# The last twelve batches of an adapter kernel, written as one list

## Chip, core and metric

The kernel runs on one core of a Trainium2 chip. The metric is the device time of one execution in microseconds (us). Five engines work beside each other, each through its own instructions in order: TensorE (PE; its weight loads are listed as PEld), VectorE (DVE), ScalarE (ACT), GpSimd (POOL), and SyncE (SP), which here issues DMA transfers. SBUF and PSUM are the core's memories: matrix products land in PSUM, GpSimd works on SBUF.

## What is computed

x has 128 batches of 128 rows and 512 columns, float32. Each batch has an id from 0 to 9 that picks its weights:

```python
h = relu(x[b] @ W1[id] + b1[id])          # 512 -> 128
y = x[b] + h @ W2[id] + b2[id]            # 128 -> 512, and the residual
n = (y - mean(y)) * rsqrt(var(y) + 1e-5)  # by row, over 512 columns
out[b] = x[b] + n * gamma[id] + beta[id]
```

## The kernel before

One batch is one tile of 128 x 512. The tables (W1, W2, and beta, gamma, b2 spread over 128 partitions as `beta_b`, `gamma_b`, `b2_b`) stay in SBUF. A batch goes through these steps; the names are those of the helpers and lines in the profile:

- TensorE transposes x in four pieces into PSUM (`transpose_x`, L271); ScalarE copies the result to SBUF (`copy_xT`, L275).
- ScalarE copies the batch's W1 out of the table into a tile (`stage_w1`, L262). Only the first 17 batches load theirs from memory by id instead (`load_first`, L161).
- TensorE makes h (`down`, L294), ScalarE adds b1 and clamps (`relu`, L302), TensorE makes h @ W2 into one of five PSUM tiles `py` (`up`, L311).
- GpSimd adds x and b2 ahead of time (`add_b2`, L281, tile `r`) and x and beta into the output tile `o` (`add_beta`, L288). For a few batches b2 comes in another way: by VectorE (L321), or by a matmul of a selecting row with the table's parts in front of the up (`b2_by_matmul`, L310: 0, 1, 126, 127).
- VectorE adds `r` or x to `py` and sums the rows (`residual`, L328). ScalarE turns the sum into a negative mean (L342) and makes the sum of squares (`square`, L351), then a first reciprocal root (`root`, L361). VectorE improves it by a Newton step in three small operations (`rstd` 1 to 3: L365, L367, L370).
- VectorE subtracts the mean and multiplies by gamma in place (`scale`, L394), and multiplies by the reciprocal root and adds `o` (`finish`, L403). SP stores two batches at once (`store`, L407).

The small steps are done for a pair of batches at a time. The tile of the root of a pair lies in PSUM, and so do those of the last four batches, which have their own (`of_one`).

Every instruction goes through `keep`, which ties it to the one issued before on its engine, so the order of the calls is the order on each engine. The loop over `i` writes that order: iteration `i` transposes batch i, makes the down of i - 1 and the up of i - 2, and does the row statistics of b = i - 3, the scaling of the pair before, and the end of the one before that. E is 123. From b = E on `tail` writes the order by hand: batches 123, 124 and 125 end by ScalarE and GpSimd instead of VectorE (`by_pool`: ScalarE scales into a tile `n`, L450; GpSimd multiplies by gamma, L452, where VectorE has not, and adds `o`, L454), and 126 and 127 end on VectorE (L461), the last in two halves. The stores of 124 and 125 are issued in halves by ScalarE, the others by SP (L457). The kernel's last instructions are at L675.

Of the kernel before, what the change touches and what calls it, by code (L numbers as in the profile page):

```python
# [22 lines left out]
U = 2  # L23
# [3 lines left out]
def cond_resid_kernel(ctx: ExitStack, tc: tile.TileContext, x, itok, W1, b1, W2, b2, gamma, beta, out):  # L27
# [286 lines left out]
    def col(tiles, b):  # L314

        return tiles[b // 2][:, b % 2 : b % 2 + 1]
# [46 lines left out]
    def newton(n, ssq, t, u):  # L363
        if n == 1:
            keep(nc.vector.scalar_tensor_tensor(u, ssq, EPS * H3, t, ALU.add, ALU.mult))  # L365
        else:
            keep(nc.vector.scalar_tensor_tensor(u, u, 1.0 / H3, t, ALU.mult, ALU.mult))  # L367

    def newton_3(rstd, t, u):
        keep(nc.vector.scalar_tensor_tensor(rstd, u, -3.0, t, ALU.add, ALU.mult))  # L370
# [28 lines left out]
    def finish(b):  # L399
        g, j = divmod(b, 2)  # L400
        o = os[g][:, j, :]
        keep(
            nc.vector.scalar_tensor_tensor(o, ys.pop(b), rstds[g][:, j : j + 1], o, ALU.mult, ALU.add)  # L403
        )

    def store(g):
        keep(nc.sync.dma_start(out=out[2 * g : 2 * g + 2].rearrange("b s h -> s b h"), in_=os.pop(g)))  # L407
        del rstds[g]

    def on(b):  # L410
        return 0 <= b < B
# [3 lines left out]
    shifts = {}  # L415
    halves = slice(0, H // 2), slice(H // 2, H)

    def of_one(b):
        if -b not in parts_of:
            pool, tag = {E + 3: (p_h, "h"), E + 4: (p_x, "xT")}.get(b, (p_s, "s"))  # L420
            parts_of[-b] = pool.tile([P, 1], FP, tag=tag, name=f"root_of_{b}"), st.tile([P, 1], FP, tag="part", name=f"part_of_{b}")
        return parts_of[-b]

    def rstd_of(b, n):

        t, u = of_one(b)
        if n < 3:
            newton(n, ssqs[b], t, u)
        else:
            rstds[b] = st.tile([P, 1], FP, tag="rstd", name=f"rstd_{b}")  # L430
            newton_3(rstds[b], t, u)

    def deviation_of(b):
        ssqs[b] = st.tile([P, 1], FP, tag="ssq", name=f"ssq_{b}")
        sq = tp.tile([P, H], FP, tag="sq", name=f"sq_{b}")
        keep(nc.scalar.activation(sq, ys[b], AF.Square, bias=col(sums, b), scale=-float(H), accum_out=ssqs[b]))  # L436
        root(ssqs[b], of_one(b)[0])

    def rstd_col(b):
        return rstds[b] if b > E else rstds[b // 2][:, b % 2 : b % 2 + 1]  # L440

    def shift(b):
        shifts[b] = st.tile([P, 1], FP, tag="shift", name=f"shift_{b}")
        keep(nc.vector.tensor_scalar(shifts[b], col(nmeans, b), rstd_col(b), None, ALU.mult))

    def by_pool(b, scaled, cols=slice(0, H)):

        n = rp.tile([P, H], FP, tag="r", name=f"n_{b}")[:, cols]
        bias = 0.0 if scaled else shifts[b]
        keep(nc.scalar.activation(n, ys[b][:, cols], AF.Identity, bias=bias, scale=rstd_col(b)))  # L450
        if not scaled:
            keep(nc.gpsimd.tensor_tensor(n, n, gamma_b[:, bass.ds(lid(b, ET.Pool) * H, H)], ALU.mult))  # L452
        for part in halves if b > E else (cols,):
            keep(nc.gpsimd.tensor_tensor(os[b // 2][:, b % 2, part], n[:, part], os[b // 2][:, b % 2, part], ALU.add))  # L454

    def store_last(b, engine=nc.sync, cols=slice(0, H)):
        keep(engine.dma_start(out=out[b][:, cols], in_=os[b // 2][:, b % 2, cols]))  # L457

    def finish_cols(b, cols=slice(0, H)):
        o = os[b // 2][:, b % 2, cols]  # L460
        keep(nc.vector.scalar_tensor_tensor(o, ys[b][:, cols], rstd_col(b), o, ALU.mult, ALU.add))  # L461

    def tail(b):
        p = E // 2
        residual(b)
        if b == E + 1:
            rstd(p, 1)
            scale(E - 1)
            rstd(p, 2)
            finish(E - 2)  # L470
            store(p - 1)
            rstd(p, 3)
            deviation_of(b)
            shift(E)
            by_pool(E, False)
        elif b == E + 2:
            rstd_of(b - 1, 1)
            negative_means(b // 2)
            rstd_of(b - 1, 2)
            finish_cols(E - 1)  # L480
            store_last(E - 1)
            rstd_of(b - 1, 3)
            store_last(E)
            deviation_of(b)
        elif b == E + 3:
            left, right = slice(0, H // 2), slice(H // 2, H)
            few, most = slice(0, H // 4), slice(H // 4, H)
            shift(b - 2)
            by_pool(b - 2, False)
            residual(b + 1)  # L490
            rstd_of(b - 1, 1)
            scale(b - 1)
            rstd_of(b - 1, 2)
            deviation_of(b)
            negative_means(b // 2)
            scale(b)
            rstd_of(b - 1, 3)
            rstd_of(b, 1)
            deviation_of(b + 1)
            rstd_of(b, 2)  # L500
            by_pool(b - 1, True)
            for part in halves:
                store_last(b - 2, nc.scalar, part)
            for part in halves:
                store_last(b - 1, nc.scalar, part)
            rstd_of(b, 3)
            rstd_of(b + 1, 1)
            finish_cols(b)
            store_last(b)
            rstd_of(b + 1, 2)  # L510
            scale(b + 1)
            rstd_of(b + 1, 3)
            for cols in (left, right):
                finish_cols(b + 1, cols)
                store_last(b + 1, nc.sync, cols)


    def spin(n, width):
        idle = p_s.tile([P, H], FP, tag="s", name="idle")
# [54 lines left out]
    up(1)  # L574

    turned = 5
    for i in range(3, B + U):
        b = i - U - 1
        if b > G and b % G == 2 and b // G + 3 < NG and b // G + 3 >= 5:
            load_x(b // G + 3)  # L580
# [20 lines left out]
        g, half = divmod(b, 2)  # L601
        p = g - 1
        mine, old = 0 <= p < B // 2, 0 <= p - 1 < B // 2
        if b == E:
            add_b2(b + 3)
            add_beta(b + 1)
            add_b2(b + 4)
            for n in range(b + 2, B):
                add_beta(n)
        if b > E:  # L610
            tail(b)
        elif half == 0:
            if on(b):
                vector_b2(b)
                residual(b)
                square(b)
            if mine:
                scale(2 * p)
                rstd(p, 1)
            if old:  # L620
                finish(2 * p - 1)
                store(p - 1)
        else:
            if on(b):
                vector_b2(b)
            if mine:
                rstd(p, 2)
            if on(b):
                residual(b)
                square(b)  # L630
            if mine:
                rstd(p, 3)
                scale(2 * p + 1)
            if mine:
                finish(2 * p)
# [44 lines left out]
```

## Time and profile before

| | |
|---|---|
| median of 3 runs | 304.56 us (304.44 to 304.68) |
| the profiled execution | 304.08 us |
| its span, first to last instruction | 302.3 us |
| busy share of PE, DVE, ACT, POOL | 96%, 97%, 92%, 94% |
| mean granted clock of TensorE | 0.993 |

The profile has one execution. Its span is what the instructions cover; 1.8 us of the time lie around it. Rows of the timeline give start, duration, engine, line, operation, out<-in and count; rows of the groups give count, busy time, mean duration in ns and the engine's idle time just before; rows of the chain of waits give start, duration and what the end was waiting for at that moment; rows of the windows give for each engine the busy time and number of instructions in a stretch. Starts of consecutive instructions of one engine can lie closer than their durations, because they overlap.

### The profile page before, as it was taken

Reading aid. Unit: us, or ns where it says so; the run is one execution under the profiler, and the core shown is the slowest. Engines: PE = TensorE matmul, PEld = TensorE weight load, DVE = VectorE, ACT = ScalarE, POOL = GpSimd, SP = SyncE. Lnnn points to the kernel's source line nnn. Section 1 sums busy time; section 2 is a strip of 40 time slices with the busy share of each in tenths; the row PEclk is TensorE's granted clock in tenths of the full one; section 3 lists DMA queues with packets and bytes.
Section 4 is the critical chain, followed back from the end, with each engine's and each line's share of the span. In section 5 each row is a group of like instructions: output and inputs, shape, how many; then the busy total and the mean of one; then the engine's idle time right before and its main releaser. Section 6 shows DMA issues by size and latency. Waiting matters only on the chain.

```text
span 302.3 us, 7001 instructions
## 1 busy us (share of the span) xinstructions
PE 290.6 (96%) x1820; PEld 218.0 (72%) x1821; DVE 294.2 (97%) x784; ACT 279.6 (92%) x771; POOL 284.9 (94%) x240
## 2 busy tenths in 40 slices
PE   7899999999999999999999999999999999999980
PEld 3758787777777777777777777777777777777740
DVE  6989999999999999999999999999999999999995
ACT  5878789999999999999999999999999999999982
POOL 1299998999999999999999999999999999999995
PEclk9999999999999999999999999999999999999997
DMA  6999999986667876766678667767866666882244
GB/s 235 385 389 364 346 339 402 404 307 206 233 234 243 279 255 205 244 209 261 222 280 270 212 204 240 263 226 261 279 211 221 218 253 217 271 283 113 108 166 173
DMA packets 43929, 77.33 MB, mean 256 GB/s; under 512 B 2121, under 2 KB 8020, under 8 KB 43890
## 3 DMA queue, kind: packets, MB, share of 16 engines
q1 hardware_dynamic: 43254, 76.31, 73.5%
q10 hardware_dynamic: 636, 0.57, 0.6%
q8 instruction: 15, 0.25, 0.3%
q14 instruction: 24, 0.20, 0.2%
HBM read 43.32 MB, written 33.55 MB: 254 GB/s over the span
## 4 chain that ended last, share of the span: by engine, by line
PE 89%; DVE 5%; DMA 2%; issue 1%; ACT 1%; SPq 0%; POOL 0%; DVEq 0%; ACTq 0%; POOLq 0%
PE ph L294 36%; PE py L311 35%; PE pxT L271 18%; DMA x<-in_x_dram 2%; DVE py L394 2%; DVE py L328 1%; DVE o L403 1%; PE row L229 1%; SPq L161 0%; ACT n L450 0%; ACT sq L351 0%; ACT sq L436 0%; DVE o L461 0%; ACT w1s L262 0%; DVE rstd L370 0%
## 5 line engine op out<-in xcount | busy, mean ns | idle before, releaser
L288 POOL TENSOR_TENSOR o<-x,beta_b 128x512 f32<-128x512 f32 x128 | 170.1, 1359 | 12.7 <-DVE beta_b L247 11.6
L294 PE MATMUL ph<-xT,w1s 128*128 128x128 f32 x1024 | 135.3, 275 | 0.2 <-DMA w1s<-in_L_cond_W_dram 0.2
L281 POOL TENSOR_TENSOR r<-x,b_b 128x512 f32<-128x512 f32 x97 | 131.7, 1360 | 0.0
L311 PE MATMUL py<-w,hT 128*128 x256 | 131.3, 595 | 0.0
L294 PEld LDWEIGHTS ph<-xT,w1s 128*128 128x128 f32 x1024 | 124.8, 192 | 1.3 <-issue 0.6
L271 PEld LDWEIGHTS pxT<-ident,x 128*128 128x128 f32 x512 | 66.0, 149 | 66.8 <-issue 49.9
L394 DVE SCALAR_TENSOR_TENSOR py<-py,nmean,gamma_b 128x512 f32<-128x512 f32 x126 | 94.8, 753 | 0.0
L403 DVE SCALAR_TENSOR_TENSOR o<-py,rstd,o 128x512 f32<-128x512 f32 x122 | 91.1, 747 | 0.0
L351 ACT ACTIVATE sq<-py,sum 128x512 f32<-128x512 f32 x124 | 85.8, 692 | 0.6 <-DVE py L328 0.6
L275 ACT COPY xT<-pxT 128x512 f32<-128x512 f32 x128 | 74.7, 583 | 4.3 <-PE pxT L271 4.1
L271 PE MATMUL pxT<-ident,x 128*128 128x128 f32 x512 | 77.6, 274 | 0.8 <-DMA x<-in_x_dram 0.6
L262 ACT COPY w1s<-w 128x512 f32 x111 | 68.0, 613 | 0.0
L328 DVE SCALAR_TENSOR_TENSOR py<-py,r 128x512 f32<-128x512 f32 x97 | 66.9, 690 | 0.2
L302 ACT ACTIVATE hT<-ph,b1T 128x128 f32<-128x128 f32 x128 | 46.9, 367 | 8.8 <-PE ph L294 4.2
L311 PEld LDWEIGHTS py<-w,hT 128*128 128x128 f32 x256 | 39.1, 192 | 1.4 <-issue 0.7
L351 ACT ACTIVATION_READ_ACCUMULATOR sq<-py,sum 128x1 f32 x124 | 25.1, 202 | 0.0
L328 DVE SCALAR_TENSOR_TENSOR py<-py,x 128x512 f32<-128x512 f32 x31 | 21.7, 699 | 1.4 <-PE py L311 1.1
L321 DVE TENSOR_TENSOR py<-py,b_b 128x512 f32<-128x512 f32 x27 | 18.6, 689 | 0.1
L361 ACT ACTIVATE root<-ssq,eps 128x2 f32<-128x2 f32 x62 | 16.5, 265 | 0.0
L328 DVE DVE_READ_ACCUMULATOR py<-py,r 128x1 f32 x97 | 13.6, 140 | 0.0
L342 ACT ACTIVATE nmean<-sum 128x2 f32<-128x2 f32 x62 | 12.3, 198 | 0.0
L365 DVE SCALAR_TENSOR_TENSOR part<-ssq,root 128x2 f32<-128x2 f32 x62 | 9.3, 149 | 0.2 <-ACT root L361 0.2
(57 smaller groups left out, 81.2 us busy)
## 6 DMA issues: line engine op xcount, KB each, us to landing
out_dram<-o SPq DMA_DIRECT2D x61, 512.0 KB, 3.3
x<-in_x_dram SPq DMA_DIRECT2D x27, 1024.0 KB, 6.7
x<-in_x_dram SPq DMA_DIRECT2D x10, 512.0 KB, 7.2
w1s<-in_L_cond_W_dram SPq DMA_DIRECT2D x17, 256.0 KB, 8.7
w<-in_L_cond_W_dram SPq DMA_DIRECT2D x4, 640.0 KB, 8.2
w<-in_L_cond_W_dram SPq DMA_DIRECT2D x1, 1792.0 KB, 9.8
w<-in_L_cond_W_dram SPq DMA_DIRECT2D x1, 768.0 KB, 5.3
out_dram<-o SPq DMA_DIRECT2D x3, 256.0 KB, 2.0
```

Source lines behind the costliest of these rows:

```text
L262: keep(nc.scalar.copy(w1s[b].rearrange("p k a -> p (k a)"), src))
L271: keep(nc.tensor.transpose(pxs[b][:, k, :], cols, ident))
L275: keep(nc.scalar.copy(xT[b], pxs.pop(b)))
L281: keep(nc.gpsimd.tensor_tensor(rs[b], xb(b), b2_b[:, bass.ds(v * H, H)], ALU.add))
L288: keep(nc.gpsimd.tensor_tensor(os[g][:, j, :], xb(b), beta_b[:, bass.ds(v * H, H)], ALU.add))
L294: nc.tensor.matmul(phs[b], lhsT=w1s[b][:, k, :], rhs=xT[b][:, k, :], start=(k == 0), stop=(k == KC - 1))
L302: keep(nc.scalar.activation(hT[b], phs.pop(b), AF.Relu, bias=b1T[:, bass.ds(lid(b, ET.Activation), 1)]))
L311: keep(nc.tensor.matmul(ys[b], lhsT=hT[b], rhs=w2[:, bass.ds(v * H, H)], start=not m, stop=True))
L328: nc.vector.scalar_tensor_tensor(ys[b], ys[b], 1.0, r, ALU.mult, ALU.add, accum_out=col(sums, b))
L351: nc.scalar.activation(sq, ys[b], AF.Square, bias=col(sums, b), scale=-float(H), accum_out=col(ssqs, b))
L394: nc.vector.scalar_tensor_tensor(ys[b], ys[b], col(nmeans, b), gamma_b[:, bass.ds(v * H, H)], ALU.add, ALU.mult)
L403: nc.vector.scalar_tensor_tensor(o, ys.pop(b), rstds[g][:, j : j + 1], o, ALU.mult, ALU.add)
```

## The change

The loop stops after b = 118, and everything from the transposition of 122 on is one list of calls, 152 lines long. In it:

- b2 of 122 comes by the matmul in front of its up, not by GpSimd.
- x + beta of 126 is made by TensorE in PSUM (`base_of`: a matmul that picks beta, and one of the identity with x), not by GpSimd; batch 126 is scaled into a tile `n` in SBUF, and its end adds the PSUM tile.
- W1 of 125, 126 and 127 is loaded from memory by id (`load_late`), not copied by ScalarE.
- 118, 123, 124 and 125 are scaled by VectorE and end by ScalarE and GpSimd (`n_of`, `add_of`); 121 is not scaled by VectorE, GpSimd multiplies by gamma (`gamma_of`). Before, 118 and 121 ended on VectorE, and 123 and 124 had gamma from GpSimd.
- The root and the three Newton operations of 124 to 127 are for one batch each, as before; the root's tile lies in SBUF (`root_of`, tag "one").
- The means of 124 and 125 are made by ScalarE, those of 126 and 127 by one small VectorE operation each.
- All stores go through SP; 122 and 123 are stored as a pair, 124, 125 and 127 in halves.
- The register loads of the ids for the last two groups stand at the head of the list.

The core of the diff, with `tail` and the functions it alone used taken out, and the list whole:

```diff
-        return b in (0, 1) or b >= B - 2
+        return b in (0, 1) or b - E in (-1, 3, 4)
...
-    def of_one(b):
...
-    def by_pool(b, scaled, cols=slice(0, H)):
...
-    def tail(b):
...
+    def beta_of(b):
+        keep(nc.gpsimd.tensor_tensor(out_of(b), xb(b), beta_b[:, bass.ds(lid(b, ET.Pool) * H, H)], ALU.add))
+    def b2_of(b):
+        rs[b] = rp.tile([P, H], FP, tag="r", name=f"r_{b}")
+        keep(nc.gpsimd.tensor_tensor(rs[b], xb(b), b2_b[:, bass.ds(lid(b, ET.Pool) * H, H)], ALU.add))
     def rstd_col(b):
+        return rstds[-b] if -b in rstds else rstds[b // 2][:, b % 2 : b % 2 + 1]
     def shift(b):
         shifts[b] = st.tile([P, 1], FP, tag="shift", name=f"shift_{b}")
         keep(nc.vector.tensor_scalar(shifts[b], col(nmeans, b), rstd_col(b), None, ALU.mult))
+    def n_of(b, scaled, cols=slice(0, H)):
+        rs[b] = rp.tile([P, H], FP, tag="r", name=f"n_{b}")
         bias = 0.0 if scaled else shifts[b]
+        keep(nc.scalar.activation(rs[b][:, cols], ys[b][:, cols], AF.Identity, bias=bias, scale=rstd_col(b)))
+    def mean_of(b, engine):
+        if b // 2 not in nmeans:
+            nmeans[b // 2] = st.tile([P, 2], FP, tag="nmean", name=f"nmean_{b // 2}")
+        if engine is nc.scalar:
+            keep(nc.scalar.activation(col(nmeans, b), col(sums, b), AF.Copy, scale=-1.0 / H))
+        else:
+            keep(nc.vector.tensor_scalar(col(nmeans, b), col(sums, b), -1.0 / H, None, ALU.mult))
+    def gamma_of(b):
+        keep(nc.gpsimd.tensor_tensor(rs[b], rs[b], gamma_b[:, bass.ds(lid(b, ET.Pool) * H, H)], ALU.mult))
+    def add_of(b, cols=slice(0, H)):
+        o = out_of(b)[:, cols]
+        keep(nc.gpsimd.tensor_tensor(o, rs[b][:, cols], o, ALU.add))
+    def square_of(b):
+        ssqs[-b] = st.tile([P, 1], FP, tag="ssq", name=f"ssq_of_{b}")
+        sq = tp.tile([P, H], FP, tag="sq", name=f"sq_{b}")
+        keep(nc.scalar.activation(sq, ys[b], AF.Square, bias=col(sums, b), scale=-float(H), accum_out=ssqs[-b]))
+    def root_of(b):
+        parts_of[-b] = st.tile([P, 1], FP, tag="one", name=f"root_of_{b}"), st.tile([P, 1], FP, tag="part", name=f"part_of_{b}")
+        root(ssqs[-b], parts_of[-b][0])
+    def rstd_of(b, n):
+        t, u = parts_of[-b]
+        if n < 3:
+            newton(n, ssqs[-b], t, u)
+        else:
+            rstds[-b] = st.tile([P, 1], FP, tag="rstd", name=f"rstd_of_{b}")
+            newton_3(rstds[-b], t, u)
+    base = {}
+    def base_of(b, pool, tag):
+        base[b] = pool.tile([P, H], FP, tag=tag, name=f"base_{b}")
+        pick_b = pick[:, bass.ds(lid(b, ET.PE), 1)].to_broadcast([96, P])
+        keep(nc.tensor.matmul(base[b], lhsT=pick_b, rhs=parts[:96, :], start=True, stop=False))
+        keep(nc.tensor.matmul(base[b], lhsT=ident, rhs=xb(b), start=False, stop=True))
+    def end_of(b, cols=slice(0, H)):
+        o = out_of(b)[:, cols]
+        keep(nc.vector.scalar_tensor_tensor(o, (rs if b in base else ys)[b][:, cols], rstd_col(b), base[b][:, cols] if b in base else o, ALU.mult, ALU.add))
+    def scale_out(b):
+        v = lid(b, ET.DVE)
+        rs[b] = rp.tile([P, H], FP, tag="r", name=f"n_{b}")
+        keep(
+            nc.vector.scalar_tensor_tensor(
+                rs[b], ys[b], col(nmeans, b), gamma_b[:, bass.ds(v * H, H)], ALU.add, ALU.mult
+            )
+        )
+    def load_late(b):
+        w1s[b] = wp.tile([P, KC, A], FP, tag="w1s", name=f"w1s_{b}")
+        src = W1[bass.ds(lid(b, ET.SP), 1)].rearrange("o (k p) a -> p (o k) a", k=KC)
+        keep(nc.sync.dma_start(out=w1s[b], in_=src))
     def store_last(b, engine=nc.sync, cols=slice(0, H)):
         keep(engine.dma_start(out=out[b][:, cols], in_=os[b // 2][:, b % 2, cols]))
+    def store_pair(g):
+        keep(nc.sync.dma_start(out=out[2 * g : 2 * g + 2].rearrange("b s h -> s b h"), in_=os[g]))
...
-    for i in range(3, B + U):
+    for i in range(3, B - 6):
...
-        if b == E:
...
-        if b > E:
-            tail(b)
-        elif half == 0:
+        if half == 0:
...
+    lid(E - 3, ET.DVE)
+    lid(E + 1, ET.DVE)
+    lid(E + 1, ET.PE)
+    lid(E + 1, ET.SP)
+    transpose_x(E - 1)
+    residual(E - 4)
+    b2_of(E - 2)
+    beta_of(E)
+    beta_of(E - 1)
+    rstd(E // 2 - 3, 2)
+    beta_of(E + 2)
+    rstd(E // 2 - 3, 3)
+    load_late(E + 3)
+    load_late(E + 2)
+    copy_xT(E - 1)
+    down(E - 2)
+    relu(E - 2)
+    square(E - 4)
+    beta_of(E + 4)
+    end_of(E - 7)
+    up(E - 3)
+    residual(E - 3)
+    scalar_means(E // 2 - 2)
+    transpose_x(E)
+    deviation(E // 2 - 2)
+    rstd(E // 2 - 2, 1)
+    down(E - 1)
+    copy_xT(E)
+    beta_of(E - 2)
+    scale(E - 6)
+    scale(E - 5)
+    transpose_x(E + 1)
+    end_of(E - 6)
+    scale(E - 4)
+    stage_w1(E)
+    rstd(E // 2 - 2, 2)
+    rstd(E // 2 - 2, 3)
+    load_late(E + 4)
+    up(E - 2)
+    residual(E - 2)
+    b2_of(E)
+    relu(E - 1)
+    down(E)
+    up(E - 1)
+    copy_xT(E + 1)
+    store_pair(E // 2 - 3)
+    end_of(E - 4)
+    transpose_x(E + 2)
+    square(E - 3)
+    stage_w1(E + 1)
+    residual(E - 1)
+    relu(E)
+    down(E + 1)
+    n_of(E - 5, True)
+    up(E)
+    add_of(E - 5)
+    square(E - 2)
+    deviation(E // 2 - 1)
+    rstd(E // 2 - 1, 1)
+    scalar_means(E // 2 - 1)
+    rstd(E // 2 - 1, 2)
+    rstd(E // 2 - 1, 3)
+    b2_of(E + 1)
+    scale(E - 3)
+    copy_xT(E + 2)
+    transpose_x(E + 3)
+    shift(E - 2)
+    relu(E + 1)
+    square(E - 1)
+    copy_xT(E + 3)
+    residual(E)
+    negative_means(E // 2)
+    down(E + 2)
+    square(E)
+    b2_of(E + 2)
+    end_of(E - 3)
+    beta_of(E + 1)
+    scale(E - 1)
+    relu(E + 2)
+    up(E + 1)
+    deviation(E // 2)
+    rstd(E // 2, 1)
+    n_of(E - 2, False)
+    residual(E + 1)
+    transpose_x(E + 4)
+    copy_xT(E + 4)
+    square_of(E + 1)
+    down(E + 3)
+    relu(E + 3)
+    rstd(E // 2, 2)
+    mean_of(E + 1, nc.scalar)
+    store_pair(E // 2 - 2)
+    root_of(E + 1)
+    rstd(E // 2, 3)
+    up(E + 2)
+    scale(E)
+    n_of(E, True)
+    end_of(E - 1)
+    gamma_of(E - 2)
+    residual(E + 2)
+    square_of(E + 2)
+    mean_of(E + 2, nc.scalar)
+    add_of(E)
+    scale(E + 1)
+    up(E + 3)
+    residual(E + 3)
+    add_of(E - 2)
+    store_pair(E // 2)
+    scale(E + 2)
+    root_of(E + 2)
+    rstd_of(E + 2, 1)
+    rstd_of(E + 1, 1)
+    mean_of(E + 3, nc.vector)
+    store_pair(E // 2 - 1)
+    rstd_of(E + 2, 2)
+    down(E + 4)
+    relu(E + 4)
+    rstd_of(E + 1, 2)
+    rstd_of(E + 2, 3)
+    rstd_of(E + 1, 3)
+    square_of(E + 3)
+    root_of(E + 3)
+    scale_out(E + 3)
+    rstd_of(E + 3, 1)
+    n_of(E + 1, True)
+    n_of(E + 2, True)
+    up(E + 4)
+    residual(E + 4)
+    square_of(E + 4)
+    rstd_of(E + 3, 2)
+    rstd_of(E + 3, 3)
+    mean_of(E + 4, nc.vector)
+    base_of(E + 3, p_h, "h")
+    end_of(E + 3)
+    root_of(E + 4)
+    scale(E + 4)
+    add_of(E + 1, halves[0])
+    store_last(E + 1, nc.sync, halves[0])
+    add_of(E + 1, halves[1])
+    store_last(E + 1, nc.sync, halves[1])
+    rstd_of(E + 4, 1)
+    add_of(E + 2, halves[0])
+    rstd_of(E + 4, 2)
+    rstd_of(E + 4, 3)
+    store_last(E + 3, nc.sync)
+    store_last(E + 2, nc.sync, halves[0])
+    end_of(E + 4, halves[0])
+    add_of(E + 2, halves[1])
+    store_last(E + 2, nc.sync, halves[1])
+    end_of(E + 4, halves[1])
+    store_last(E + 4, nc.sync, halves[0])
+    store_last(E + 4, nc.sync, halves[1])
```

More of the change, by code (lines that the diff above doesn't have):

```diff
@@ L402, in finish @@
         keep(
[L403 removed]
+            nc.vector.scalar_tensor_tensor(o, ys[b], rstds[g][:, j : j + 1], o, ALU.mult, ALU.add)
         )
@@ L463, in tail @@
-    def tail(b):
[L464 to L515, printed above, removed]
@@ L603, in cond_resid_kernel @@
         mine, old = 0 <= p < B // 2, 0 <= p - 1 < B // 2
-        if b == E:
[L605 to L609, printed above, removed]
-        if b > E:
-            tail(b)
-        elif half == 0:
+        if half == 0:
             if on(b):
```

31 lines of the change are left out of this document (4 added, 27 removed).

## Prediction

> **What bounds the kernel now.** I read the page first (shares, then the chain of waits), then the chain, the timeline and the groups of the last 25 us.
>
> ```profile
> PE 290.6 (96%) x1820; PEld 218.0 (72%) x1821; DVE 294.2 (97%) x784; ACT 279.6 (92%) x771; POOL 284.9 (94%) x240
> ...
> PE 89%; DVE 5%; DMA 2%; issue 1%; ACT 1%; SPq 0%; POOL 0%; DVEq 0%; ACTq 0%; POOLq 0%
> ```
>
> Over the whole span TensorE carries the chain. The change leaves everything before batch 119 alone, though, so what matters is the chain of the last stage:
>
> ```profile
> 276.37 0.86 PE py L311 x2
> ...
> 277.67 0.89 PE ph L294 x8
> 278.56 0.86 PE py L311 x2
> ...
> 279.89 0.75 DVE py L328 x2
> ...
> 297.48 0.67 DVE py L394
> ```
>
> Two ups lie 278.56 - 276.37 = 2.19 us apart: TensorE's pace for one batch. From 279.9 on, the chain leaves TensorE and passes along VectorE, with short stops at ScalarE. The same stretch by busy time (PE, PEld, DVE, ACT, POOL, then clock, DMA share, GB/s):
>
> ```profile
> 277.82:299.20 21.38, 15.65 (x93) 10.92 (x91) 20.68 (x65) 18.07 (x51) 20.40 (x19) 0.98 0.38 146
> 294.50:298.50 4.00, 0.00 (x0) 0.00 (x0) 3.65 (x14) 2.41 (x7) 3.92 (x6) 0.98 0.32 118
> 298.50:301.00 2.50, 0.00 (x0) 0.00 (x0) 0.70 (x2) 0.00 (x0) 0.29 (x1) 0.50 0.97 335
> ```
>
> 277.82 is where the new list begins on VectorE, 299.20 where VectorE ends. It is busy for 20.68 of 21.38 us; GpSimd is nearly as full, TensorE is done early. The third row is the second bound: for the last 2.5 us the DMA engines are full (0.97). So the end is VectorE's last result, and then a queue of stores.
>
> **The change, part by part: VectorE.** Its work in the stretch, by group:
>
> ```profile
> L394 DVE SCALAR_TENSOR_TENSOR py<-py,nmean,gamma_b 128x512 f32<-128x512 f32 x9 | 6.8, 754 | 0.0
> L403 DVE SCALAR_TENSOR_TENSOR o<-py,rstd,o 128x512 f32<-128x512 f32 x7 | 5.2, 746 | 0.0
> L328 DVE SCALAR_TENSOR_TENSOR py<-py,r 128x512 f32<-128x512 f32 x7 | 4.8, 691 | 0.1
> L461 DVE SCALAR_TENSOR_TENSOR o<-py,rstd,o 128x512 f32<-128x512 f32 (+1 forms) x4 | 2.4, 613 | 0.2
> L328 DVE SCALAR_TENSOR_TENSOR py<-py,x 128x512 f32<-128x512 f32 x2 | 1.4, 696 | 0.0
> L365 DVE SCALAR_TENSOR_TENSOR part_of<-ssq,root_of 128x1 f32<-128x1 f32 x4 | 0.6, 149 | 0.0
> ```
>
> So 9 residuals, 9 scalings, 8 whole ends (six on L403, the seventh there being that of 115, which reaches into the stretch; 122 and 126 on L461), two half ends, and 27 small operations (23 Newton steps, two means, two shifts). Instructions overlap, so I cost them by the distance between starts:
>
> ```profile
> 281.95 0.69 DVE L328 SCALAR_TENSOR_TENSOR py<-py,r 128x512 f32<-128x512 f32 x1
> ...
> 282.56 0.15 DVE L370 SCALAR_TENSOR_TENSOR rstd<-part,root 128x2 f32<-128x2 f32 x1
> 282.62 0.75 DVE L394 SCALAR_TENSOR_TENSOR py<-py,nmean,gamma_b 128x512 f32<-128x512 f32 x1
> 283.29 0.75 DVE L403 SCALAR_TENSOR_TENSOR o<-py,rstd,o 128x512 f32<-128x512 f32 x1
> 283.95 0.69 DVE L328 SCALAR_TENSOR_TENSOR py<-py,r 128x512 f32<-128x512 f32 x1
> ```
>
> Residual 0.61, small 0.06 to 0.07, scaling 0.67, end 0.66. Before: 9 x 0.61 + 9 x 0.67 + 8 x 0.66 + 27 x 0.07 + 0.40 + 0.48 for the halves = 19.6 of 21.4 us; 1.8 us is stall. The list has 9 residuals again, 10 scalings (123 and 124 come back from GpSimd, 121 goes there), 6 whole ends (116, 117, 119, 120, 122, 126; those of 118 and 121 go to ScalarE and GpSimd), the halves, and again 27 small operations (23 Newton steps, three means, one shift). Work: 0.67 - 2 x 0.66 = **-0.65 us**.
>
> The stalls decide whether that arrives. A small operation that reads the one right before it costs more:
>
> ```profile
> 296.04 0.15 DVE L365 SCALAR_TENSOR_TENSOR part_of<-ssq,root_of 128x1 f32<-128x1 f32 x1
> 296.22 0.16 DVE L367 SCALAR_TENSOR_TENSOR part_of<-part_of,root_of 128x1 f32<-128x1 f32 x1
> 296.41 0.15 DVE L370 SCALAR_TENSOR_TENSOR rstd<-part_of,root_of 128x1 f32<-128x1 f32 x1
> ...
> 298.06 0.15 DVE L370 SCALAR_TENSOR_TENSOR rstd<-part_of,root_of 128x1 f32<-128x1 f32 x1
> 298.32 0.88 DVE L461 SCALAR_TENSOR_TENSOR o<-py,rstd,o 128x256 f32<-128x256 f32 x2
> ```
>
> 0.18 to 0.19 instead of 0.07: 0.12 lost each time, and 0.26 - 0.07 = 0.19 ahead of the first half end. In the new order eleven places are like that (pair 58 two, 59 one, 60 two, the mean of pair 61, 61 one, 126 one, 127 two and its half end): 1.3 us. About 0.35 more goes on ends and scalings right behind them, which wait for a second engine as at 298.32, and 0.15 on pair 60's root and the up of 123. That is 1.8 again: the waits of before (pair 61's root, the up of 124, shifts) are filled, and the bare Newton chains take their place. VectorE then ends at 299.20 - 0.65 = 298.55.
>
> **The other engines.** ScalarE:
>
> ```profile
> L262 ACT COPY w1s<-w 128x512 f32 x5 | 3.1, 611 | 0.0
> ...
> L450 ACT ACTIVATE n<-py,rstd 128x512 f32<-128x512 f32 x1 | 0.7, 668 | 0.0
> ```
>
> Three of five W1 copies go (-1.83), two more normalised results come (+1.4, 118 and 121) and a mean more. It is 18.07 of 21.38 us busy: hidden; if the cover were gone, +0.2 at most shows.
>
> ```profile
> L310 PE MATMUL py<-parts,pick 96*128 96x512 bf16 x4 | 1.5, 380 | 0.0
> L311 PE MATMUL py<-w,hT 128*128 x256 | 131.3, 595 | 0.0
> ```
>
> TensorE gets one 0.38 for b2 of 122 and 0.38 + 2 x 0.595 for beta of 126, the latter behind its last up, in a stage where the second window shows it idle: hidden. The first delays the ups by at most 0.38, and in the layout residuals 124 to 127 come 0.5 to 0.8 after their ups: hidden. The new waits of TensorE are two: the up of 123 takes its PSUM tile from an end that now runs on ScalarE (118) or VectorE (119), both some 0.8 earlier, and the base of 126 waits for the last relu, with nothing of TensorE behind it.
>
> GpSimd loses two additions (b2 of 122, beta of 126) and two gammas, and gains 118's addition and gamma and addition of 121: one fewer.
>
> ```profile
> 279.15 1.45 POOL L281 TENSOR_TENSOR r<-x,b_b 128x512 f32<-128x512 f32 x1
> 280.39 1.45 POOL L288 TENSOR_TENSOR o<-x,beta_b 128x512 f32<-128x512 f32 x1
> ...
> 294.68 1.26 POOL L452 TENSOR_TENSOR n<-n,gamma_b 128x512 f32<-128x512 f32 x1
> 296.02 2.77 POOL L454 TENSOR_TENSOR o<-n,o 128x256 f32<-128x256 f32 x4
> ```
>
> They follow each other at 1.23 (279.15 to 280.39), and the one at 279.15 is in third place. The addition of 118, in eighth place, now stands ahead of b2 of 124, 125 and beta of 124: if ScalarE's result for 118 were late, those would be, and with them residuals 124 and 125. In the layout it is there at 284, the eighth place at 285.3. b2 of 124 is in ninth place, 279.15 + 6 x 1.23 = 286.5, done at 288.0; residual 124 comes at 288.5. The last four half additions (2.77) wait for the results of 124 and 125 and end near 297.6, ahead of VectorE: hidden.
>
> **The stores.** All the last ones move to SP, in order:
>
> ```profile
> 299.26 0.40 SPq L457 DMA_DIRECT2D out_dram<-o  x1
> ```
>
> ```profile
> w1s<-in_L_cond_W_dram SPq DMA_DIRECT2D x17, 256.0 KB, 8.7
> ...
> out_dram<-o SPq DMA_DIRECT2D x3, 256.0 KB, 2.0
> out_dram<-o ACTq DMA_DIRECT2D x4, 128.0 KB, 2.2
> ```
>
> A 128 KB store takes longer than one of 256 KB: it stands in the queue that the third window shows. At 335 GB/s 128 KB are 0.39 us and 256 KB 0.78, so alone it would take about 2.0 - 0.4 = 1.6 to 1.7: 0.4 is queue. In the list the stores of 124 go out about a microsecond earlier, and from 126's on 0.78 + 4 x 0.39 meet 1.9 us of issues: the queue is gone, **-0.4**. Bounds: 0 and -0.5. What SP gains, seven issues of up to 0.40, fits between the results. In its order the second half of 125 stands ahead of both halves of 127: should GpSimd end after 298.1, each 0.1 of that delays the end by 0.1; it has 0.5 to spare.
>
>
> ```profile
> 277.93 13.33 SPq L407 DMA_DIRECT2D out_dram<-o  x4
> ```
>
> The three W1 loads are issued behind this store, of pair 57, by about 279.1 for 125 (a register load and issues of 0.4). The down at 277.67 in the chain above is that of 121; four batches and b2 of 122 later, 277.7 + 4 x 2.19 + 0.2 = 286.6, that of 125 needs its weights. The nearest rows are 2.0 (a store of that size in the quiet stage) and 8.7 (loads into a full queue); I take the first, as the DMA share here is 0.38: hidden.
>
> **The sum.** -0.65 - 0.4 = -1.05 us on the profiled execution's 304.08 (span 302.3, 1.8 around it), that is 303.0; the median of the runs is 304.56, 0.48 higher, so **303.5**. By stalls of 1.8 +- 0.3 and the store bounds: 303.1 to 304.0.
>
> **One cost the trace does not show.** The roots of 124 to 127 move from PSUM to SBUF, so their 12 Newton steps read two SBUF tensors while GpSimd works on SBUF. No VectorE row of the last stage does.
>
> ```profile
> L91 DVE MEMSET warm<- 128x1 f32 x1 | 0.1, 59 | 0.8 <-PEq L666 0.8
> ```
>
> Bounds: below, 0.09 saved on each of six chained ones if they come down to this smallest row (-0.5); above, each waits for the GpSimd instruction under way, 0.69 to 1.26. I take the nearest row, 0.149, the same operation with one operand in PSUM.
>
> [...]
>
> **Rivals.** (1) *Newton steps wait for GpSimd.* By the pitches, step 1 of 125 is due after 8 residuals, 8 scalings, 5 ends, 13 small operations and 1.1 of stalls: 277.82 + 4.88 + 5.36 + 3.30 + 0.91 + 1.08 = 293.35. The additions of 123 and 121 start when ScalarE has 123's result, near 291.5, and run to 291.5 + 2 x 1.23 = 294.0: 0.6 of waiting; steps 2 and 3 of 126 are due after the four half additions have begun, 0.3 and 0.7 if the engines take turns. Total 1.6: **305.1 to 305.2**, slower. If the four additions (2.77) hold VectorE in one piece, 306.4. It turns the sign from 1.05 us of waiting. For: GpSimd is full; against: no row. (2) *The list only trades.* Bare chains cost 0.1 more at each of eleven places, or the store queue stays: 304.3. For: the count of chains; against: 0.12 is measured. (3) *W1 late.* At 8.7 us the load of 125 lands at 287.8, 1.2 behind its down, of which VectorE's lag takes 0.5 and the store queue's loss comes back: 304.7; at the 10 us that two such loads in a row would mean, 305.6. Against: the DMA share.
>
> **Chances.** Forecast 0.43, rival 1 0.40, rival 2 0.14, rival 3 0.03. A measurement tells about 0.2% (0.6 us) from no change. Faster: 0.40 of the forecast and 0.01 of rival 1 (little waiting) = 0.41. Same: 0.03, 0.12 and 0.13 of the first three = 0.28. Slower: 0.27 of rival 1 (0.15 by turns, 0.12 in the long form), 0.01 and 0.03 = 0.31. The range, 303.0 to 305.7, leaves out the long form and the best edge; the forecast's own is 303.1 to 304.0.
>
> **What would show it.** Right: VectorE's last end 0.65 earlier, small operations of 0.15, the last 128 KB stores landing in 1.7, DMA share under 0.8 at the end. Wrong: Newton rows of 0.5 or more or idle before them while GpSimd adds; TensorE waiting for W1.

## The result, and the profile after

The changed kernel takes 304.84 us, median of 22 runs (304.54 to 305.80), beside 304.43 for the kernel before in the same comparison (22 runs, 304.01 to 304.68). The ratio is 1.0017, 95% interval 1.0012 to 1.0023: 0.17% slower, where 303.5 was forecast. The profiled execution of the changed kernel took 304.56 us with a span of 302.8; that of before took 304.08 with 302.3.

The page, busy times and the chain by engine:

```profile
PE 293.4 (97%) x1825; PEld 219.6 (73%) x1825; DVE 294.7 (97%) x783; ACT 279.6 (92%) x771; POOL 283.5 (94%) x239
...
PE 84%; DVE 10%; issue 3%; DMA 1%; ACT 0%; DVEq 0%; ACTq 0%
```

VectorE's share of the chain went from 5% to 10%. That is not the list's doing alone: in this execution the chain leaves TensorE for good near 258 us, 20 us ahead of the list, where the two kernels are the same. So the shares of the whole span decide nothing, and the last stage has to be read by itself. Its windows (PE, PEld, DVE, ACT, POOL, clock, DMA share, GB/s):

```profile
277.82:299.65 21.83, 17.28 (x98) 11.69 (x96) 21.31 (x64) 18.02 (x51) 18.96 (x18) 1.00 0.54 189
294.50:298.50 4.00, 0.91 (x3) 0.08 (x1) 3.90 (x11) 2.34 (x5) 2.77 (x4) 1.00 0.68 255
298.50:301.00 2.50, 0.00 (x0) 0.00 (x0) 1.07 (x4) 0.00 (x0) 0.00 (x0) 0.69 0.86 306
```

VectorE ends at 299.65 instead of 299.20, and is busy for 21.31 us instead of 20.68, although its list holds less work. Where that busy time sits, the groups of the stage show (count, busy time, mean ns):

```profile
L370 DVE SCALAR_TENSOR_TENSOR rstd_of<-part_of,root_of 128x1 f32<-128x1 f32 x4 | 1.0, 278 | 0.1
...
L365 DVE SCALAR_TENSOR_TENSOR part_of<-ssq_of,root_of 128x1 f32<-128x1 f32 x4 | 0.8, 230 | 0.0
...
L367 DVE SCALAR_TENSOR_TENSOR part_of<-part_of,root_of 128x1 f32<-128x1 f32 x4 | 0.7, 184 | 0.0
```

These are the 12 Newton operations of 124 to 127, which took 149 ns each at L365 before. At most 0.1 us of waiting is listed before them: the time is inside the instructions. The timeline says when:

```profile
291.52 2.50 POOL L454 TENSOR_TENSOR o<-n,o 128x512 f32<-128x512 f32 x2
292.29 0.69 DVE L328 SCALAR_TENSOR_TENSOR py<-py,x 128x512 f32<-128x512 f32 x1
...
293.56 0.55 DVE L365 SCALAR_TENSOR_TENSOR part_of<-ssq_of,root_of 128x1 f32<-128x1 f32 x2
...
295.35 2.77 POOL L454 TENSOR_TENSOR o<-n,o 128x256 f32<-128x256 f32 x4 [1.34 <-ACT n L439]
...
295.81 0.29 DVE L367 SCALAR_TENSOR_TENSOR part_of<-part_of,root_of 128x1 f32<-128x1 f32 x1
...
296.13 0.64 DVE L370 SCALAR_TENSOR_TENSOR rstd_of<-part_of,root_of 128x1 f32<-128x1 f32 x1
...
298.77 0.87 DVE L483 SCALAR_TENSOR_TENSOR o<-py,rstd_of,o 128x256 f32<-128x256 f32 x2
299.28 0.82 SPq L500 DMA_DIRECT2D out_dram<-o  x2
```

GpSimd's two whole additions end at 291.52 + 2.50 = 294.02; the first operation of the pair at 293.56 ends at 294.03. The half additions take 0.72 and follow each other at 0.68, so the first ends at 296.07 and the second at 296.75; the steps at 295.81 and 296.13 end at 296.09 and 296.77. By their own records these three operations last 478, 286 and 644 ns, each until 16 to 18 ns behind the end of a GpSimd instruction, where 149 was forecast: 0.33 + 0.14 + 0.49 = 0.96 us. The other nine of the 12, made while GpSimd idles or has all but ended, take 0.14 to 0.16.

The second difference lies behind the last store. SyncE's waits at the end, kernel before and then changed kernel (total us, times, longest):

```profile
SPq L675 <- DMA out_dram<-o: 1.2, 3, 0.7
```

```profile
SPq L807 <- DMA out_dram<-o: 1.4, 1, 1.4
```

In the traces the record of each transfer names one of eight semaphores: the 137 transfers of the changed kernel take the eight in turn, as a ring, and so do the 135 of the kernel before, but for its last stores, which two engines issue beside each other. The last store has landed at 301.38 before and at 301.47 after, and SyncE's wait for its semaphore is through at 301.40 and 301.48. SyncE ends with one wait for each of the eight, in the same order in both traces and 0.06 to 0.07 us apart where it has not to wait. Before, the last store was on the seventh: SyncE waited three times, and of the eight only the last was left when the store landed. In the changed kernel the store is on the first: one wait of 1.4, and seven others still to go through. From the landing to the end of the span, called the tail below, it is 0.95 before and 1.33 after.

The transfers themselves, issue to landing:

```profile
w1s<-in_L_cond_W_dram SPq DMA_DIRECT2D x3, 256.0 KB, 3.6
```

```profile
out_dram<-o SPq DMA_DIRECT2D x6, 128.0 KB, 1.8
```

The account, by the two traces: the whole loop runs 0.12 later in this execution; VectorE's work and other stalls -0.63, which here is what is left over once the other terms are taken off; the three steps +0.96; from VectorE's end to the last landing 1.82 instead of 2.18, -0.36; the tail +0.38. That is +0.47, as far as the spans of 302.80 and 302.33 lie apart.

### The profile page after: what moved, and what is told of

It is laid out like the page before. It is cut to its first block, busy times and chain, and to the rows that moved or that the text cites. A ratio compares the mean times of both kernels' runs of the same rounds, so it can differ in the third digit from the quotient of the medians.

```text
span 302.8 us, 7016 instructions
## 1 busy us (share of the span) xinstructions
PE 293.4 (97%) x1825; PEld 219.6 (73%) x1825; DVE 294.7 (97%) x783; ACT 279.6 (92%) x771; POOL 283.5 (94%) x239
## 4 chain that ended last, share of the span: by engine, by line
PE 84%; DVE 10%; issue 3%; DMA 1%; ACT 0%; DVEq 0%; ACTq 0%
PE ph L294 33%; PE py L311 32%; PE pxT L271 17%; DVE py L328 3%; DVE py L394 3%; DVE o L483 1%; PE row L229 1%; DMA out_dram<-o 1%; DVE o L403 1%; DMA rows<-in_L_cond_b_dram 1%; DVE rstd_of L370 0%; PE idle L509 0%; DVE part L367 0%; DVE n L489 0%; DVE part L365 0%
## 5 line engine op out<-in xcount | busy, mean ns | idle before, releaser
L288 POOL TENSOR_TENSOR o<-x,beta_b 128x512 f32<-128x512 f32 x121 | 154.7, 1292 | 12.7 <-DVE beta_b L247 12.7
L281 POOL TENSOR_TENSOR r<-x,b_b 128x512 f32<-128x512 f32 x92 | 119.0, 1293 | 0.0
L403 DVE SCALAR_TENSOR_TENSOR o<-py,rstd,o 128x512 f32<-128x512 f32 x116 | 86.6, 746 | 0.0
L328 DVE SCALAR_TENSOR_TENSOR py<-py,r 128x512 f32<-128x512 f32 x96 | 66.2, 689 | 0.1
L262 ACT COPY w1s<-w 128x512 f32 x108 | 66.2, 613 | 0.0
L328 DVE SCALAR_TENSOR_TENSOR py<-py,x 128x512 f32<-128x512 f32 x32 | 22.4, 699 | 0.6 <-PE py L311 0.2
L370 DVE SCALAR_TENSOR_TENSOR rstd<-part,root 128x2 f32<-128x2 f32 x62 | 9.3, 150 | 0.2
```

The costliest lines, as they stand in the source:

```text
L262: keep(nc.scalar.copy(w1s[b].rearrange("p k a -> p (k a)"), src))
L281: keep(nc.gpsimd.tensor_tensor(rs[b], xb(b), b2_b[:, bass.ds(v * H, H)], ALU.add))
L288: keep(nc.gpsimd.tensor_tensor(os[g][:, j, :], xb(b), beta_b[:, bass.ds(v * H, H)], ALU.add))
L328: nc.vector.scalar_tensor_tensor(ys[b], ys[b], 1.0, r, ALU.mult, ALU.add, accum_out=col(sums, b))
L403: nc.vector.scalar_tensor_tensor(o, ys[b], rstds[g][:, j : j + 1], o, ALU.mult, ALU.add)
```

## The experiments

The theory: the three long steps, each with two SBUF tensors as inputs, wait for the GpSimd instruction under way (0.33, 0.14 and 0.49 us), and the order of SyncE's last waits adds the rest (0.38). The rival: the long steps are waits of another kind that end beside GpSimd's by chance, and the list itself trades nothing for nothing. Each kernel below is compared with the kernel before on its own chip; that one took 304.22, 304.35 and 304.35 us in the three series.

### Roots back in PSUM

```diff
     def root_of(b):
-        parts_of[-b] = st.tile([P, 1], FP, tag="one", name=f"root_of_{b}"), st.tile([P, 1], FP, tag="part", name=f"part_of_{b}")
+        if not roots:
+            roots[0] = p_x.tile([P, 4], FP, tag="xT", name="roots")
+        c = b - E - 1
+        parts_of[-b] = roots[0][:, c : c + 1], st.tile([P, 1], FP, tag="part", name=f"part_of_{b}")
         root(ssqs[-b], parts_of[-b][0])
...
-    base = {}
+    base, roots = {}, {}
```

> The changed kernel with the roots of 124 to 127 in PSUM again (four columns of one tile in the bank of the transposes, which is free by then), so that each of their 12 Newton steps reads one SBUF tensor and one PSUM tensor. Theory (a Newton step with two SBUF inputs waits for the GpSimd instruction under way, 0.33 + 0.14 + 0.49 = 0.96 us in the profile): all steps at 0.14 to 0.16, the three long ones gone, time 0.9 us lower, 303.9. Rival (the long steps are waits for something else, a semaphore or the order of the list, and merely end near GpSimd's instructions): they stay, 304.8. A third case, that the shared tile brings waits of its own between ScalarE's roots and the steps: 304.2 to 304.6 with idle time before steps, not long steps.

303.98 us, ratio 0.9987 (0.9977 to 0.9998) to the kernel before, where the changed kernel had 1.0017: 0.30%, 0.9 us. The groups and two rows of the timeline:

```profile
L370 DVE SCALAR_TENSOR_TENSOR rstd_of<-part_of,roots 128x1 f32<-128x1 f32 x4 | 0.5, 154 | 0.1
L367 DVE SCALAR_TENSOR_TENSOR part_of<-part_of,roots 128x1 f32<-128x1 f32 x4 | 0.5, 150 | 0.0
L365 DVE SCALAR_TENSOR_TENSOR part_of<-ssq_of,roots 128x1 f32<-128x1 f32 x4 | 0.5, 148 | 0.0
```

```profile
292.50 0.69 DVE L328 SCALAR_TENSOR_TENSOR py<-py,x 128x512 f32<-128x512 f32 x1
...
298.02 0.88 DVE L486 SCALAR_TENSOR_TENSOR o<-py,rstd_of,o 128x256 f32<-128x256 f32 x2
```

From residual 126 to VectorE's end it is 298.90 - 292.50 = 6.40 us; in the changed kernel 299.64 - 292.29 = 7.35. The difference of 0.95 is the sum of the three waits. GpSimd's additions stand beside the steps as before, and the steps now run at 0.15 in the middle of them, so the rival falls. Not all of the 0.95 reaches the end: the last store lands 2.12 behind VectorE here, and 1.82 in the changed kernel, so the traces show 0.65 of it at the last landing. The 0.9 of the medians is known to about 0.4 and fits both.

### One store fewer

```diff
     add_of(E + 1, halves[0])
-    store_last(E + 1, nc.sync, halves[0])
     add_of(E + 1, halves[1])
-    store_last(E + 1, nc.sync, halves[1])
+    store_last(E + 1, nc.sync)
```

> The changed kernel with the two half stores of 124 as one whole store (256 KB, three microseconds ahead of the end), so that the last store of all gets the next semaphore back in the ring of eight. Theory (SyncE's eight last waits run in a fixed order of about 0.065 us each, and the last store of the changed kernel sits on the first of them): the last store is now the last one waited for, the time from landing to the end of the span falls from 1.34 to about 0.9, and the time by 0.4 to 304.4. Rival (the longer tail is something else of the end): 304.8. The long Newton steps stay in both cases.

304.14 us, ratio 0.9997 (0.9983 to 1.0011). Against 1.0017 that is 0.6 us less, a little more than the 0.4 expected, with an interval that holds 0.4. The trace shows the mechanism:

```profile
SPq L806 <- DMA out_dram<-o: 0.9, 2, 0.5
```

The last store is on the last of the eight, the other seven are through before it lands, and from landing to the end of the span it is 0.89 us, not 1.33. The three long steps are still there, with 0.54, 0.29 and 0.65.

### Both edits

> Both edits at once. Theory: the two are independent, 0.9 + 0.4 = 1.3 us lower, 303.5, which is 0.9 below the kernel before, and VectorE ends near 298.7 of its span. If the two share a cause, or the store queue comes back when VectorE ends earlier: 303.9 or more. If the rearranged list itself only trades, 304.0 to 304.4.

303.56 us, ratio 0.9978 (0.9967 to 0.9989): 0.66 us below the kernel before, where this experiment expected 0.9 and the prediction 1.05, and faster than both kernels. That the time itself comes out at the 303.5 that both named is luck: the kernel before takes 304.22 here and took 304.56 when the prediction was made. The sum behind the number did not come:

```profile
296.82 2.79 SPq L503 DMA_DIRECT2D out_dram<-o  x6
...
298.00 0.88 DVE L486 SCALAR_TENSOR_TENSOR o<-py,rstd_of,o 128x256 f32<-128x256 f32 x2
```

VectorE ends at 298.87, with a loop that runs 0.31 later than in the trace of before: 0.64 earlier, as forecast. The last store, though, is issued at 299.22 and lands at 301.06, 2.19 behind VectorE's end, as far as in the kernel before (2.18). The 0.4 us of store queue that the forecast counted as gone are back, as the second case of this experiment had it, though that case put the time at 303.9 or more.

### Which queue it is

```diff
-    store_last(E + 2, nc.sync, halves[1])
+    store_last(E + 2, nc.scalar, halves[1])
...
-    store_last(E + 4, nc.sync, halves[0])
+    store_last(E + 4, nc.scalar, halves[0])
```

> The kernel with both edits (roots in PSUM, one store fewer), and of its last four half stores two on ScalarE's queue, the second of 125 and the first of 127, so that SyncE does not issue all of them. In the profile with both edits SyncE issues at 298.22, 298.72 and 299.22, 0.50 apart, and the last issue comes 0.36 after VectorE's end at 298.87. Theory (SyncE's issues have become the bound): the last issue follows VectorE by 0.06 and the time falls by 0.3, to 303.25. Rival (the transfers wait in the DMA engines anyway): 303.5.

303.55 us, ratio 0.9977 (0.9968 to 0.9986): no change. The stretch from 298.7 to 302, in 40 slices of 0.08 us with the busy share of the DMA engines in tenths, first with all stores on SyncE and then here, and the issues here with the time to landing:

```profile
DMA  9988999899999999989998830000000000000000
```

```profile
DMA  9988999999989998989996100000000000000000
...
out_dram<-o ACTq DMA_DIRECT2D x1, 128.0 KB, 2.0
out_dram<-o SPq DMA_DIRECT2D x1, 128.0 KB, 2.2
```

The last issue now follows VectorE's end by 0.03 us, but takes 2.15 to land instead of 1.84. The theory fell: SyncE's pitch of 0.50 was a limit beside another one. The DMA engines are at 80% or more until 300.6 in the first and until 300.5 in the second. Six stores, 1 MB in all, are issued here between 296.7 and 298.8; at the 335 GB/s of the full DMA engines in the prediction's window they take 3.1 us by estimate, one more than that. With only the roots in PSUM, where 124 is still stored in halves, the last landing is 2.12 behind VectorE too, so the merged store isn't the cause.

### The roots in SBUF alone, in the kernel before

```diff
-            pool, tag = {E + 3: (p_h, "h"), E + 4: (p_x, "xT")}.get(b, (p_s, "s"))
-            parts_of[-b] = pool.tile([P, 1], FP, tag=tag, name=f"root_of_{b}"), st.tile([P, 1], FP, tag="part", name=f"part_of_{b}")
+            parts_of[-b] = st.tile([P, 1], FP, tag="one", name=f"root_of_{b}"), st.tile([P, 1], FP, tag="part", name=f"part_of_{b}")
```

> The kernel before with that part of the change alone: the roots of 124 to 127 in SBUF, nothing else. Theory: steps that fall into GpSimd's additions wait for the end of the one under way; by the trace of before, step 1 of 125 (at 294.13, in a GpSimd instruction that ends at 294.73) waits 0.45, step 2 (in the next, to 295.95) about 0.5, and the later ones up to 0.6 each in the halves of 0.72: 1.0 to 1.8 us slower, 305.4 to 306.2. Rival (two SBUF inputs cost nothing): 304.3 to 304.5.

305.90 us, ratio 1.0049 (1.0031 to 1.0066): 1.7 us slower by the medians, in the upper half of what was expected. The three groups:

```profile
L370 DVE SCALAR_TENSOR_TENSOR rstd<-part_of,root_of 128x1 f32<-128x1 f32 x4 | 1.8, 438 | 0.0
L367 DVE SCALAR_TENSOR_TENSOR part_of<-part_of,root_of 128x1 f32<-128x1 f32 x4 | 1.6, 412 | 0.0
...
L365 DVE SCALAR_TENSOR_TENSOR part_of<-ssq,root_of 128x1 f32<-128x1 f32 x4 | 0.6, 151 | 0.0
```

The excess over 0.15 is 4 x 0.29 + 4 x 0.26 = 2.2 us. Not all of it is in the time: a part covers other waits, and with VectorE later the last store lands 1.85 behind it instead of 2.18. Which steps are hit had been guessed wrong: step 3 of 124 already waited, so step 1 of 125 came when GpSimd was all but done, and steps 2 and 3 of 125 and step 2 of 127 paid.

### The same in the whole loop

```diff
-            parts_of[g] = p_s.tile([P, 2], FP, tag="s", name=f"root_{g}"), st.tile([P, 2], FP, tag="part", name=f"part_{g}")
+            parts_of[g] = st.tile([P, 2], FP, tag="two", name=f"root_{g}"), st.tile([P, 2], FP, tag="part", name=f"part_{g}")
```

> The kernel before with the roots of all 62 pairs of the loop in SBUF instead of PSUM: 186 Newton steps with two SBUF inputs, beside a GpSimd that is busy 94% of the span in instructions of 1.29 us. Theory (each such step waits for the GpSimd instruction under way): 0.6 us on average for 186 steps is 110 us of waiting at most; VectorE can give back little, being busy 97%, while GpSimd idles more as the loop stretches, so 50 to 110 us slower: 355 to 415. Mean of the steps about 0.6 instead of 0.15. Rival (no wait): 304.2 to 304.6.

377.22 us in one run, 72.9 more than the kernel before. Lines of its page:

```profile
PE 316.8 (84%) x1821; PEld 226.6 (60%) x1821; DVE 367.4 (98%) x784; ACT 289.1 (77%) x771; POOL 286.1 (76%) x240
...
L281 POOL TENSOR_TENSOR r<-x,b_b 128x512 f32<-128x512 f32 x97 | 123.8, 1276 | 68.9 <-DVE py L328 39.9
...
L367 DVE SCALAR_TENSOR_TENSOR part<-part,root 128x2 f32<-128x2 f32 x62 | 39.3, 634 | 0.0
L365 DVE SCALAR_TENSOR_TENSOR part<-ssq,root 128x2 f32<-128x2 f32 x62 | 38.8, 625 | 0.0
L370 DVE SCALAR_TENSOR_TENSOR rstd<-part,root 128x2 f32<-128x2 f32 x62 | 25.2, 406 | 0.0
```

186 operations on two columns take 103.3 us instead of 186 x 0.15 = 27.9: 75.4 us more, and nearly all of it is in the time. 113 of the 186 take more than 0.2 us, and every one of these ends 15 to 23 ns behind the end of a GpSimd instruction; that is no chance. A wait for the GpSimd instruction under way fits in size too: by estimate from its share of 76% and its mean of 1.28 us, an operation that meets GpSimd at a random moment finds it busy in 76% of cases and then waits for half of 1.28, 0.49 on average over all cases, and steps 1 and 2 take 0.63, 0.48 more than alone. Step 3 follows step 2 closely and waits for 0.26.

### The other side of the wait

Two kernels with both edits. In the first GpSimd adds beta of 126 again:

```diff
+    beta_of(E + 3)
     store_pair(E // 2)
...
-    scale_out(E + 3)
+    scale(E + 3)
...
-    base_of(E + 3, p_h, "h")
```

> The kernel with both edits, but beta of 126 added by GpSimd again (one addition of 1.23 us behind that of 121, where GpSimd otherwise idles for 1.17 us until ScalarE's result for 124), its scaling in PSUM and no sum on TensorE. Theory (that part of the change is hidden): 303.4 to 303.7, the half additions of 124 and 125 begin at most 0.1 later. Rival (GpSimd's late additions bound the last stores): 303.9 or more.

In the second, the scaled result of 126 stays in SBUF all the same (`scale_out` kept, and the end reads it and `o`):

> As the kernel with beta of 126 by GpSimd, but the scaled result of 126 goes to SBUF, so that its end (128x512) reads two SBUF tensors while GpSimd makes the half additions. Theory (whoever comes second waits): the end waits 0 to 0.7 us for the addition under way, and the next addition of GpSimd waits for the whole end, about 0.7: 303.8 to 304.6, and here GpSimd too shows a long instruction or a gap. Rival (only VectorE ever waits): GpSimd's additions stay 0.68 apart. Second rival (no wait for large instructions): 303.5.

The first took 303.71 us, ratio 0.9978 (0.9970 to 0.9987): that edit of the change is worth nothing measurable. The second took 304.32, ratio 1.0001 (0.9988 to 1.0013), with a wide spread (303.71 to 305.66): 0.6 more, as the theory expected. The four half additions and the end of 126, first kernel and then second:

```profile
295.12 2.80 POOL L454 TENSOR_TENSOR o<-n,o 128x256 f32<-128x256 f32 x4
295.81 0.75 DVE L486 SCALAR_TENSOR_TENSOR o<-py,rstd_of,o 128x512 f32<-128x512 f32 x1
```

```profile
295.10 3.23 POOL L454 TENSOR_TENSOR o<-n,o 128x256 f32<-128x256 f32 x4
...
295.82 1.24 DVE L486 SCALAR_TENSOR_TENSOR o<-n,rstd_of,o 128x512 f32<-128x512 f32 x1
```

The end takes 1.24 instead of 0.75, because GpSimd's second half addition, begun at 295.78, had come first; and the third half addition, begun while the end held VectorE, takes 1.18 by its own record instead of 0.76, and the fourth begins 1.15 behind it instead of 0.68. Both sides wait. The Newton operations of 0.15 had cost GpSimd nothing that its pitch of 0.68 shows.

### Two transfers more, in the kernel before

```diff
-            load_x(b // G + 3)
+            g = b // G + 3
+            if g in (10, 14):
+                xs[g] = xp.tile([P, G, H], FP, tag="x", name=f"x_{g}")
+                load_part(g * G, g * G + 2)
+                load_part(g * G + 2, g * G + 4)
+            else:
+                load_x(g)
```

> The kernel before with two loads of x in mid-loop split into halves: two transfers more, which moves its last store from the last but one of SyncE's eight final waits to the first of them, and nothing else near the end. Theory (what comes after the landing depends on where in that order the last store stands): 0.92 us from landing to the end becomes about 1.3, time +0.35 to +0.45, 304.6. Rival (the order of the waits costs nothing): 304.2, as the kernel before on this chip.

304.68 us, ratio 1.0012 (1.0003 to 1.0021): 0.33 by the medians, just under the 0.35 to 0.45 that was expected.

```profile
SPq L681 <- DMA out_dram<-o: 1.7, 1, 1.7
```

One long wait again, and 1.33 us from landing to the end, by two loads split a hundred microseconds or more ahead of it. The last store lands 2.18 behind VectorE, as in the kernel before, so the tail alone has changed.

### W1 and b2 the old way

With both edits, W1 of 125 to 127 copied by ScalarE:

```diff
-    load_late(E + 3)
-    load_late(E + 2)
...
-    load_late(E + 4)
...
     relu(E)
+    stage_w1(E + 2)
...
     relu(E + 1)
+    stage_w1(E + 3)
...
     square_of(E + 1)
+    stage_w1(E + 4)
...
-    store_pair(E // 2 - 3)
+    store_last(2 * (E // 2 - 3))
+    store_last(2 * (E // 2 - 3) + 1)
```

(and so the next two pairs).

> The kernel with both edits, but W1 of 125 to 127 copied by ScalarE again instead of loaded late, three copies of 0.61 us, and three stores of pairs split so that the count of transfers and the last waits stay. Theory (ScalarE is hidden at 18 of 21 us): 0 to 0.2, 303.5 to 303.75, ScalarE 1.8 us busier in the last stage. Rival (ScalarE's squares and roots of the last batches come late by its full queue, and the loads are what the change lives on): 304 or more, with VectorE idle ahead of residuals or steps.

304.34 us, ratio 1.0000 (0.9991 to 1.0009), 0.8 more than with the loads (303.55 on the same chip, the kernel with stores on two queues). The rival was right. 282 to 290 us with both edits, and then here:

```profile
282.00:290.00 8.00, 8.00 (x53) 6.17 (x52) 7.74 (x25) 7.81 (x22) 8.00 (x7) 1.00 0.54 189
```

```profile
282.00:290.00 8.00, 7.98 (x52) 5.95 (x51) 7.50 (x23) 7.97 (x22) 8.00 (x8) 1.00 0.27 102
```

and who waits there:

```profile
PEld py L311 <- ACT hT L302: 1.3, 1, 1.3
...
DVE part L365 <- ACT root L361: 0.3, 1, 0.3
```

ScalarE, 18.0 of 21 us busy over the whole stage, was full in this part of it already (7.81 of 8): the copies make relus and roots late, and VectorE waits for them and for later ups. The three places of the copies were mine; others may cost less.

With both edits, b2 of 122 by GpSimd:

```diff
-        return b in (0, 1) or b - E in (-1, 3, 4)
+        return b in (0, 1) or b - E in (3, 4)
...
     b2_of(E - 2)
+    b2_of(E - 1)
```

> The kernel with both edits, but b2 of 122 added by GpSimd again, as second of the list. Theory (GpSimd is full from 278 to 294, so what stands behind is 1.23 later): b2 of 124 ends at 289.3 instead of 288.05, residual 124 waits 0.3 for it, 303.8 to 304.0. Rival (GpSimd's idle time ahead of the half additions hides it): 303.5.

303.96 us, ratio 0.9992 (0.9982 to 1.0002): as expected, 0.25 to 0.4 above the kernels with b2 by the matmul, though the intervals overlap. Residual 124 comes at 289.17, and with both edits alone at 288.95, in a loop that runs 0.09 later there: 0.31 later, and VectorE's end is 0.32 later.

## Why the prediction was wrong

The forecast was 1.05 us less; by the medians 0.41 more came.

- **VectorE's work and stalls.** Forecast -0.65, measured -0.63, and -0.64 in the kernel with both edits, where the three waits are gone. The mechanism was right too: counted with the prediction's own pitches (the distances between starts), the stretch has 1.8 us of stall before, 1.8 with both edits and 2.8 in the changed kernel, and the difference of 1.0 sits on the three long steps.
- **"One cost the trace does not show": the step that failed.** Between 0.149 and a wait for GpSimd the prediction took the nearest row, an operation with one operand in PSUM. That row could not tell the two apart, since the operand's place is what decides: with the root in PSUM the three groups of steps take 0.15 on average (first experiment), and with it in SBUF, in the kernel before, L367 and L370 take 0.41 and 0.44. No row of before showed such a wait. The runs put 0.96 us there. Rival 1, which the prediction had given a chance of 0.40 beside the forecast's 0.43, had it: it named the same three operations (step 1 of 125, steps 2 and 3 of 126) with 0.6, 0.3 and 0.7, measured 0.33, 0.14 and 0.49, in turns and not in one piece. Its waits came out too long because its start of the first was 0.2 early and because it counted each operation's own 0.15 as wait.
- **The tail.** The prediction added the same 1.8 around the span and the same time behind the last landing. The change makes two transfers more than before, the last store moved from the seventh to the first of the eight waits, and +0.38 came from that. No row quoted in the prediction showed the waits behind the landing; the waits of SyncE would have.
- **The store queue.** -0.36 came, against a forecast of -0.4, but that is luck: it came for a reason that the prediction did not give, that VectorE was late. Where VectorE waits, the last store lands 1.82 to 1.85 behind it (the changed kernel, the one with a store fewer, the kernel before with its roots in SBUF). Where it does not, the queue is back (2.1 to 2.2), whoever issues the stores. So this term and the waits belong together: of their 0.96 us, some 0.6 reach the end. The DMA share at the end, foreseen under 0.8, was 0.86.
- **What was hidden.** The loads of W1 were, and so was beta of 126. But the cost of a load was too low: that of 125 stands behind that of 126 in the list and was issued at 279.67, not 279.1, and took 3.6 us, not the 2.0 of the nearest row. It landed at 283.23, and its down began at 286.60, so the slack of 3.4 us covered it. GpSimd's last addition ended at 298.12 instead of 297.6, which used up the spare of 0.5 without costing anything. The reverse, "if the cover were gone, +0.2 at most" for ScalarE, was wrong: 0.8 with the copies put back.
- **The list.** It does not only trade: without the two costs it is 0.66 us faster, and taking back b2 of 122 alone costs 0.3 to 0.4 of that, the W1 loads alone 0.8.

## What to carry to other kernels

Before moving a small operand from PSUM to SBUF, look what else its instruction reads, and whether GpSimd is busy then: here three of the changed kernel's 12 operations of 0.15 us, with two SBUF tensors as inputs, lasted until GpSimd's instruction had ended, 0.29 to 0.64 us. A busy share over a stage of 20 us does not say what an engine can take in a part of it; cut the stage into windows first. And when the time behind the last store moves without cause, count the transfers: the place of the last one among SyncE's eight last waits was worth 0.3 to 0.4 us here (0.33 by the medians of the run with two transfers more, 0.38 by the traces of the change).

## What the hardware showed besides

The long operations of the changed kernel end 16 to 18 ns behind GpSimd's instruction, and between two GpSimd instructions that follow each other without a gap VectorE gets its turn: step 3 of 126 ends at 296.77, while the next half addition, begun at 296.72, runs to 297.44. So it does in the run with all roots in SBUF, with one exception among the 113 long steps: one lasts 3.62 us, through three GpSimd instructions in a row; why is open. Not every second column in SBUF counts: `shift` reads two, the mean as its tensor and the reciprocal root as its scalar, one value per row. In the kernel before one `shift` runs from 290.95 to 291.17, in the middle of a GpSimd addition (290.24 to 291.70), in 0.21 us, and so without a wait. Steps 1 and 2 on two columns (0.63 us, with all roots in SBUF) cost nearly as much as a scaling of 128x512 (0.75). With both edits SyncE's last three issues start 0.50 us apart (298.22, 298.72 and 299.22); in the changed kernel two start 0.48 apart (298.07 and 298.55), and the first of them is listed with 0.38.
